# A token stage put into the kernel's own list schedule, with longer two-operand VectorE instructions in place of turns at a shared port

## The chip, the cores and the metric

The kernel runs on one core of a Trainium2 chip. A core has five engines with a queue of instructions each: TensorE (PE in the profile, with its weight loads as PEld), VectorE (DVE), ScalarE (ACT), GpSimd (POOL) and SyncE (SP), which here only starts DMAs. An engine takes its instructions in the order in which the program lists them for it, and waits for another engine through semaphores. On-chip memory is SBUF, and PSUM, which TensorE writes its products to. The metric is the time of one execution on the device in microseconds (us).

## The reference

Four layers are applied in turn to 64 images of 128 channels and 28 x 28 pixels, all in float32: a block of two quantised 3x3 convolutions, self-attention over the pixels, a Mamba layer over the sequence of pixels, and a token Mamba. Only the last is touched. It cuts the 128 channels of each pixel into 8 tokens of 16 channels, and runs a small Mamba over these 8 tokens, for each pixel apart (32 inner channels d, 16 states s):

```
seq = x.transpose(0, 2, 3, 1).reshape(B * H * W, TOKEN_NUM, D_MODEL)
# _mamba(seq): after projection, convolution over the tokens and silu
dt  = softplus(dt @ dt_proj_w.T + dt_proj_b)
dA  = exp(dt[..., None] * A)
dBx = dt[..., None] * Bm[:, :, None, :] * xs[..., None]
h   = dA_t * h + dBx_t                    # step over the 8 tokens
y_t = einsum('nds,ns->nd', h, C_t)
y   = (y + xs * D) * silu(z);  out = y @ out_proj_w.T
```

Then a group norm over 4 groups of channels, silu, and the sum with x.

## The kernel before

The program has three parts one after the other: `conv_block`, `attention_and_mamba` and `token_mamba`. The second already computes the inputs of the token Mamba: xs (`utd`) and silu(z) (`ztd`) are written to device memory for each image.

`token_mamba` has 28 groups k of 14 x 128 pixels. A group is worked in two halves dh of 16 inner channels, and a half in four blocks i of 4 channels (`DB`): 56 halves, 224 blocks. Pixels lie on the 128 partitions, and the free dimension of a block's tile is 4 channels x 16 states x 14 pixel columns = 896 elements.

For each group, `x_proj` (line 1184) computes B and C for all 8 tokens into the tile `BC`: row loads (line 1179), matmuls into `bank` and `dt` (lines 1197 and 1203), copies by ScalarE, a product by VectorE (line 1212) and its sum by TensorE (line 1215). For each half, `delta_u` makes `delta` (softplus) and `u` (delta times xs): 16 ScalarE operations, transposes (line 1242) with copies, four ScalarE passes over 1792 elements, two VectorE passes (lines 1258, 1259), two GpSimd passes (lines 1262, 1263), and `diag` by VectorE (line 1266).

For each block, `exps` fills `a`, the decays of tokens 1 to 7, with 64 ScalarE exponentials of 98 elements. All calls of ScalarE carry line 235 in the profile, that of a helper. `a` has two buffers. `block` runs the recurrence with the state `h` in PSUM, one buffer: GpSimd makes the seven inputs `db` (line 1296, five buffers) and two products (lines 1307 and 1309); VectorE makes the first `h` (line 1308) and then, token by token, multiplies by `a` (line 1311), multiplies by C into `a` or `late` (line 1313) and adds `db` (line 1315). TensorE sums over the states into `y` (lines 1318, 1320 and 1322), ScalarE copies `y` to `ysb`. For each half, `gate` transposes back (line 1333), gates with VectorE and GpSimd (lines 1338 and 1339), exchanges halves through memory (`ygd`), projects (line 1347) and copies to the image `xr` (line 1357). `finish_image` does the group norm and the rest for images that are complete.

The loop at the end of `token_mamba` writes these parts down interleaved: pieces of the last half's `gate`, of the next group's `x_proj` and the next half's `delta_u`, the exponentials of the next block, then the block itself. The order on each engine is made from this by the framework's own scheduler (`tile.TileContext(nc, schedule_with_timeline_sim=True)`).

`attention_and_mamba` is ordered otherwise. There every call goes to a `Plan`, which records it as a `Step`. `add` finds what a step depends on from the parts of tiles that it reads and writes, `cost` (line 372) gives it a duration in us, a lag until others see the result, and whether it takes the port that VectorE and GpSimd share. `order` (line 399) is a list schedule: each engine picks, among its first 32 ready steps by rank, the first that can start within a given patience of the soonest; steps under `first()` have their rank lowered by a lead. A shared step can't start before the last shared step has ended (`port`): these are the turns. Buffers are taken in the order of the program, except PSUM tiles named `bank`. `issue` runs it for 12 pairs of lead and patience (`TRIED`), takes the shortest, and writes the instructions down in that order (line 479), as they are to stay.

Of the kernel before, what the change touches and what calls it, by code (L numbers as in the profile page):

```python
# [19 lines left out]
ALU = mybir.AluOpType  # L20
# [245 lines left out]
class Plan:  # L266
# [12 lines left out]
    def __init__(self, tc):  # L279
        self.tc = tc  # L280
        self.steps, self.access, self.slots, self.group, self.leading = [], {}, {}, None, False
        for e in self.ENGINES:
            setattr(self, e, Recorder(self, e))
# [88 lines left out]
    def cost(self, engine, method, outs, ins, args, kw):  # L372
# [5 lines left out]
        if engine == "tensor":  # L378
            if kw.get("is_transpose"):
                return 0.18, False, 0.25  # L380
            if outs[0].partition_size() == 32 or ins[0].partition_size() == 16:
                return 0.03 + 0.0005 * n, False, 0.25
            return 0.06 + 0.0023 * n, False, 0.25
        if engine == "gpsimd":
            return 0.2 + 0.0023 * n, True, 0.07
        if engine == "scalar":
            if not outs:
                return 1.28, False, 0.07
            a = outs[0]
            us = 0.2 + 0.00093 * n * (1.8 if len(a.ap) > 2 and abs(a.ap[-1][0]) > 1 else 1.0)  # L390
            return us + (0.2 if "accum_out" in kw else 0.0), False, 0.07
        two = len([a for a in big if a.space == SBUF]) > 1
        if method == "tensor_tensor_scan":
            return 0.18 + (0.0024 if two else 0.0021) * n, False, 0.07
        if method == "tensor_scalar" and outs[0].space == SBUF:
            return 0.14 + 0.00053 * n, True, 0.07
# [101 lines left out]
def attention_and_mamba(tc, tables, x, c2d, s2, b2x15, x2d, utd, ztd, pk3, pk4, vec, v, ident, eps):  # L498
# [11 lines left out]
    with ExitStack() as ctx:  # L510
# [99 lines left out]
        plan = Plan(tc)  # L610
# [473 lines left out]
def token_mamba(tc, tables, x2d, utd, ztd, pk4, v, ident, eps, out, NB):  # L1084
# [17 lines left out]
    with ExitStack() as ctx:  # L1102
        dram = ctx.enter_context(dram)
        wp = ctx.enter_context(tc.tile_pool(name="w4", bufs=1))
# [3 lines left out]
        ap = ctx.enter_context(tc.tile_pool(name="a4", bufs=2))  # L1108
        p2 = ctx.enter_context(tc.tile_pool(name="p4", bufs=2))
        p1 = ctx.enter_context(tc.tile_pool(name="p4b", bufs=1))  # L1110
        db = ctx.enter_context(tc.tile_pool(name="db4", bufs=5))
        cp = ctx.enter_context(tc.tile_pool(name="c4", bufs=4))
        xrp = ctx.enter_context(tc.tile_pool(name="xr4", bufs=4))
        ps = ctx.enter_context(tc.tile_pool(name="ps4", bufs=3, space=PSUM))
        psd = ctx.enter_context(tc.tile_pool(name="psd4", bufs=1, space=PSUM))
        psh = ctx.enter_context(tc.tile_pool(name="psh4", bufs=1, space=PSUM))
        psy = ctx.enter_context(tc.tile_pool(name="psy4", bufs=2, space=PSUM))
# [13 lines left out]
        act = tables.act  # L1131
        act(A, w("Alog"), AF.Exp)
        nc.vector.tensor_scalar(A, A, -1.0, None, ALU.mult)

# [5 lines left out]
        def finish_image(b):  # L1140
            xo = xr.pop(b)
            stats = p2.tile([C, 2, 6], F32, name="stats")
            for h in range(2):
                nc.vector.bn_stats(stats[:, h, :], xo[:, h * HT : (h + 1) * HT])
            mv = p2.tile([C, 2], F32, name="mv")
            nc.vector.bn_aggr(mv, stats.rearrange("p n s -> p (n s)"))
            acc = bank()
            nc.tensor.matmul(acc[:, 0:1], lhsT=grp, rhs=mv[:, 0:1], start=True, stop=True)
# [5 lines left out]
            nc.tensor.matmul(acc2[:, 0:1], lhsT=grp, rhs=sm[:, 1:2], start=True, stop=True)  # L1154
# [6 lines left out]
            nc.sync.dma_start(res, x2d[b])  # L1161
# [7 lines left out]
            nc.gpsimd.tensor_tensor(xo, xo, e, ALU.mult)  # L1169
            nc.gpsimd.tensor_tensor(res, res, xo, ALU.add)  # L1170
            nc.sync.dma_start(out[b], res)

        def load_rows(src, k, dh, g, n):
# [3 lines left out]
            for b in range(lo // T, (hi - 1) // T + 1):  # L1177
                p, q = max(lo, b * T), min(hi, (b + 1) * T)
                nc.sync.dma_start(t[:, p - lo : q - lo], src[b][:, dh, p - b * T : q - b * T])
# [4 lines left out]
        def x_proj(k):  # L1184
# [5 lines left out]
            for g, n in chunks:  # L1190
                uts = [load_rows(utd, k, dh, g, n) for dh in range(2)]
                for g2 in range(0, n, 2):
                    two = bank()
                    for j in range(2):
                        at = slice((g2 + j) * C, (g2 + j + 1) * C)
                        for dh in range(2):
                            nc.tensor.matmul(  # L1197
                                two.rearrange("p (c j) -> p c j", j=2)[:, :, j],
                                lhsT=uts[dh][:, at], rhs=w("BDx", dh * 256, (dh + 1) * 256),
                                start=(j == 0 and dh == 0), stop=(j == 1 and dh == 1),  # L1200
                            )
                        for dh in range(2):
                            nc.tensor.matmul(  # L1203
                                dt_ps[:, :, g + g2 + j], lhsT=uts[dh][:, at], rhs=w("BDt", dh * NK, (dh + 1) * NK),
                                start=(g + g2 + j == 0 and dh == 0), stop=(g + g2 + j == G - 1 and dh == 1),
                            )
# [3 lines left out]
            nc.vector.tensor_copy(small[:, 0].rearrange("p t g -> p (t g)"), acc[:, : NK * G])  # L1210
            prod = p1.tile([C, NK, NS, G], F32, name="w1")
            nc.vector.tensor_tensor(prod, BC[:, :, :NS, :], BC[:, :, NS:, :], ALU.mult)
            acc = bank()
            for i in range(NS):
                nc.tensor.matmul(
                    acc[:, : NK * G].rearrange("p (t g) -> p t g", g=G), lhsT=ident, rhs=prod[:, :, i, :],
                    start=(i == 0), stop=(i == NS - 1),
                )
            nc.vector.tensor_copy(small[:, 1].rearrange("p t g -> p (t g)"), acc[:, : NK * G])
# [7 lines left out]
        def delta_u(k, dh):  # L1227
# [9 lines left out]
            for g, n in chunks:  # L1237
# [3 lines left out]
                for j in range(n):  # L1241
                    nc.tensor.matmul(
                        acc4[:, :, j], lhsT=ut[:, j * C : (j + 1) * C], rhs=ident, is_transpose=True,
                        start=(j == 0), stop=(j == n - 1), skip_group_check=True,
                    )
# [12 lines left out]
            nc.vector.scalar_tensor_tensor(e_, w_, 1.0, e_, ALU.subtract, ALU.subtract)  # L1258
            nc.vector.scalar_tensor_tensor(v_, v_, 0.0, e_, ALU.max, ALU.subtract)
            yield  # L1260
            act(w_, w_, AF.Ln)
            nc.gpsimd.tensor_tensor(v_, v_, w_, ALU.add)
            nc.gpsimd.tensor_tensor(u_, v_, u_, ALU.mult)
            yield
            diag = p1.tile([C, NK, ND, G], F32, name="diag")
            nc.vector.tensor_tensor(diag, u, of_tg(small[:, 1]), ALU.mult)
            half[k, dh] = delta, u, diag

        def exps(k, dh, i):
            delta = half[k, dh][0]  # L1270
            a = ap.tile([C, NK - 1, DB, NS, G], F32, name="a")
            for d in range(DB):
                for n in range(NS):
                    col = (dh * ND + i * DB + d) * NS + n
                    act(a[:, :, d, n, :], delta[:, 1:, i * DB + d, :], AF.Exp, scale=A[:, col : col + 1])
            return a

        def block(k, dh, i, a, ysb):
# [15 lines left out]
            def inject(t):  # L1294
                x = db.tile([C, DB, NS, G], F32, name="db")
                nc.gpsimd.tensor_tensor(  # L1296
# [10 lines left out]
            nc.gpsimd.tensor_tensor(flat(at(1)), flat(at(1)), flat(h0), ALU.mult)  # L1307
            nc.vector.tensor_tensor(h, flat(at(1)), flat(inject(1)), ALU.add)  # L1308
            nc.gpsimd.tensor_tensor(by_d(at(1)), by_d(at(1)), Cc(1), ALU.mult)  # L1309
            for t in range(2, NK):  # L1310
                nc.vector.tensor_tensor(h, h, flat(at(t)), ALU.mult)  # L1311
                dst = at(t) if t < 6 else late[:, t - 6]
                nc.vector.tensor_tensor(by_d(dst), h_d, Cc(t), ALU.mult)  # L1313
                if t < NK - 1:
                    nc.vector.tensor_tensor(h, h, flat(inject(t)), ALU.add)  # L1315
            y = psy.tile([C, 512], F32, name="y")[:, : NK * DG]
            y3 = y.rearrange("p (t d g) -> p t d g", d=DB, g=G)
            nc.tensor.matmul(y3, lhsT=ident, rhs=diag[:, :, ds, :], start=True, stop=False)
            for n in range(NS):
                nc.tensor.matmul(y3[:, 1:6], lhsT=ident, rhs=a[:, 0:5, :, n, :], start=False, stop=False)  # L1320
            for n in range(NS):
                nc.tensor.matmul(y3[:, 6:8], lhsT=ident, rhs=late[:, :, :, n, :], start=False, stop=(n == NS - 1))  # L1322
            return y3, ysb[:, :, ds, :]

        def gate(k, dh, ysb):

            yf = ysb.rearrange("p t d g -> p (t d) g")
            for g, n in chunks:
# [3 lines left out]
                for j in range(n):  # L1332
                    nc.tensor.matmul(
                        acc[:, j * C : (j + 1) * C], lhsT=yf[:, :, g + j], rhs=ident, is_transpose=True,
                        start=(j == 0), stop=(j == n - 1), skip_group_check=True,
                    )
                yg = cp.tile([C, 512], F32, name="yg", bufs=3)
                nc.vector.scalar_tensor_tensor(yg[:, :m], ut[:, :m], v("DT", dh), acc[:, :m], ALU.mult, ALU.add)
                nc.gpsimd.tensor_tensor(yg[:, :m], yg[:, :m], zt[:, :m], ALU.mult)
                if dh == 0:  # L1340
                    nc.sync.dma_start(ygd[k % 2][:, g * C : g * C + m], yg[:, :m])
                else:
                    yg0 = cp.tile([C, 512], F32, name="yg", bufs=3)
                    nc.sync.dma_start(yg0[:, :m], ygd[k % 2][:, g * C : g * C + m])
                    acc = bank()
                    for i, r in enumerate((yg0, yg)):
                        nc.tensor.matmul(  # L1347
                            acc[:, :m], lhsT=w("BDo", i * C, (i + 1) * C), rhs=r[:, :m], start=(i == 0), stop=(i == 1)
                        )
                    lo = k * PX + g * C  # L1350
                    at = lo
                    while at < lo + m:
# [4 lines left out]
                        nc.vector.tensor_copy(xr[b][:, o : o + c], acc[:, at - lo : at - lo + c])  # L1357
# [19 lines left out]
        for q, (k, dh) in enumerate(halves_):  # L1377
# [4 lines left out]
            for i in range(NBLK):  # L1382
# [11 lines left out]
                y, dst = block(k, dh, i, a, ysb)  # L1394
                act(dst, y, AF.Copy)
# [3 lines left out]
        for _ in ends:  # L1399
            pass  # L1400

# [100 lines left out]
```

## Time and profile before

| | us |
|---|---|
| runs before, median of 3 | 14057.9 (14039.58 to 14059.44) |
| the profiled execution | 14058.7 |
| its span, first to last instruction | 14056.9 |
| token stage, first to last start of line 1308 | 7984.7 to 13985.3 |

| engine | busy us | share of the span |
|---|---|---|
| PE | 10623.3 | 76% |
| DVE | 12350.4 | 88% |
| ACT | 10874.1 | 77% |
| POOL | 11465.4 | 82% |

A profile line of a group reads: line, engine, operation, output tile <- input tiles, output shape <- input shape, number of instructions | busy us, mean ns of one | idle us of the engine just before them <- who ended it. A line of waits reads: engine and instruction that waited <- whom it waited for: us in total, number of times, longest. A line of the view of one source line or tile has the shortest, median and longest duration in ns and the first and last start. A float32 matmul appears as two records, and neighbouring instructions of ScalarE and TensorE overlap, so that the mean of one is longer than busy time over count.

### The profile page before, as it was taken

What the parts mean: (1) busy time and instruction counts of PE and PEld (TensorE: products, weight loads), DVE (VectorE), ACT (ScalarE), POOL (GpSimd) and SP (SyncE); (2) the same over time, 40 slices, a digit from 0 to 9 for tenths busy, and PEclk for the clock granted to TensorE, in tenths of its full rate; (3) what the DMA queues carried; (4) which work ended last, traced back from release to release, by engine and by line L of the source; (5) the groups of instructions that cost most, each with busy time, mean ns of one, the idle gap of its engine ahead of it and who ended that gap; (6) DMA issues with size and microseconds to landing.
All of it is one profiled execution on the core that took longest, in us unless ns stands there. A gap on an engine that the chain in (4) does not pass through costs nothing. (4 is left out here: it accounts for less than half of the span.)

```text
span 14056.9 us, 183402 instructions
## 1 busy us (share of the span) xinstructions
PE 10623.3 (76%) x59522; PEld 7022.5 (50%) x59522; DVE 12350.4 (88%) x12760; ACT 10874.1 (77%) x25936; POOL 11465.4 (82%) x5304
## 2 busy tenths in 40 slices
PE   9978777777777777777777567767767677677776
PEld 5544444444444444444443356555556555565564
DVE  3459999999999999999999788888888888888897
ACT  2357877777777777777777688888888888888886
POOL 0028999888888888898989788888888888888887
PEclk9988888888888888888888788888888888787887
DMA  2434444444444444444443211111111111111111
GB/s 102 147 111 125 126 124 128 130 126 123 123 134 125 121 126 130 129 121 125 130 127 117 77 47 57 46 50 57 49 54 48 52 58 46 49 58 49 52 49 48
DMA packets 711523, 1297.78 MB, mean 92 GB/s; under 512 B 206624, under 2 KB 357536, under 8 KB 710560
## 3 DMA queue, kind: packets, MB, share of 16 engines
q1 hardware_dynamic: 710560, 1286.05, 30.2%
q8 instruction: 469, 7.68, 0.2%
q14 instruction: 494, 4.05, 0.1%
HBM read 954.72 MB, written 330.76 MB: 91 GB/s over the span
## 5 line engine op out<-in xcount | busy, mean ns | idle before, releaser
L235 ACT ACTIVATE a<-delta,A 128x98 f32<-128x98 f32 x14336 | 3966.8, 380 | 512.7 <-PE y L1320 454.2
L479 POOL TENSOR_TENSOR h<-ur,Br 128x784 f32<-128x784 f32 x1920 | 4196.5, 2211 | 148.8 <-PE y L479 133.6
L1296 POOL TENSOR_TENSOR db<-u,BC 128x896 f32<-128x896 f32 x1568 | 3337.2, 2144 | 548.4 <-DVE h L1315 531.0
L1320 PE MATMUL y<-a,ident 128*128 128x280 f32 x7168 | 2083.5, 452 | 815.3 <-DVE a L1313 811.5
L479 DVE TENSOR_TENSOR_SCAN ah<-ah,h 128x392 f32<-128x392 f32 x2304 | 2305.0, 1000 | 60.2 <-ACT ah L479 49.0
L1320 PEld LDWEIGHTS y<-a,ident 128*128 128x128 f32 x7168 | 1549.1, 220 | 1371.4 <-POOL db L1296 582.9
L479 DVE TENSOR_TENSOR_SCAN h<-a,h 128x784 f32<-128x784 f32 x768 | 1935.6, 2525 | 99.8 <-ACT a L479 50.2
L479 ACT ACTIVATE ah<-dr,A 128x392 f32<-128x392 f32 x2304 | 1326.3, 589 | 615.1 <-DVE ah L479 601.4
L479 POOL TENSOR_TENSOR h<-h,Cr 128x784 f32<-128x784 f32 x640 | 1361.4, 2131 | 356.1 <-DVE h L479 349.2
L1311 DVE TENSOR_TENSOR h<-h,a 128x896 f32<-128x896 f32 x1344 | 1475.4, 1098 | 39.0
L479 DVE TENSOR_TENSOR h<-ah,Cr 128x392 f32<-128x392 f32 x2304 | 1303.7, 566 | 72.9
L479 PE MATMUL y<-h,fold 128*32 128x98 f32 (+1 forms) x12288 | 1019.9, 421 | 396.7 <-DVE h L479 370.4
L1315 DVE TENSOR_TENSOR h<-h,db 128x896 f32<-128x896 f32 x1120 | 1230.1, 1098 | 68.0 <-POOL db L1296 0.5
L479 PEld LDWEIGHTS bank<-vt,et 112*112 112x112 f32 x6272 | 890.8, 212 | 233.8 <-ACT et L479 91.8
L1313 DVE TENSOR_TENSOR a<-h,BC 128x896 f32<-128x896 f32 x896 | 976.1, 1089 | 25.5
L479 PE MATMUL bank<-vt,et 112*112 112x128 f32 x6272 | 966.3, 317 | 5.1 <-ACT et L479 3.0
L479 POOL TENSOR_TENSOR xn<-s,sq 128x784 f32<-128x784 f32 x64 | 135.9, 2123 | 1017.3 <-ACT sq L479 961.3
L1322 PEld LDWEIGHTS y<-late,ident 128*128 128x128 f32 x7168 | 839.5, 192 | 38.9 <-DVE late L1313 20.6
L1322 PE MATMUL y<-late,ident 128*128 128x112 f32 x7168 | 844.4, 274 | 16.7 <-DVE late L1313 16.6
L479 PEld LDWEIGHTS y<-h,fold 128*32 128x32 f32 x12288 | 379.3, 121 | 923.8 <-DVE h L479 439.2
L479 ACT ACTIVATE a<-dr,A 128x784 f32<-128x784 f32 x768 | 718.6, 944 | 154.2 <-DVE h L479 152.5
L1308 DVE TENSOR_TENSOR h<-a,db 128x896 f32<-128x896 f32 x224 | 394.1, 1759 | 388.4 <-POOL a L1307 381.0
(213 smaller groups left out, 20996.5 us busy)
## 6 DMA issues: line engine op xcount, KB each, us to landing
Br<-bcd SPq DMA_DIRECT2D x1536, 98.0 KB, 2.4
Cr<-bcd SPq DMA_DIRECT2D x1536, 98.0 KB, 2.4
dr<-dud SPq DMA_DIRECT2D x1280, 98.0 KB, 2.3
ur<-dud SPq DMA_DIRECT2D x1280, 98.0 KB, 2.3
utd<-tok SPq DMA_DIRECT2D x128, 392.0 KB, 2.7
ztd<-tok SPq DMA_DIRECT2D x128, 392.0 KB, 3.7
rows<-utd SPq DMA_DIRECT2D x192, 256.0 KB, 2.7
xt<-in_x SPq DMA_DIRECT2D x32, 784.0 KB, 4.4
```

The lines of the kernel that those rows point to most:

```text
L235: ins = self.tc.nc.scalar.activation(*args, **kw)
L479: last = getattr(getattr(nc, engine), method)(*args, **kw)
L1296: nc.gpsimd.tensor_tensor(x, of_dg(du[:, t, ds, :]), BC[:, t, :NS, :].unsqueeze(1).broadcast_to([C, DB, NS, G]), ALU.mult)
L1308: nc.vector.tensor_tensor(h, flat(at(1)), flat(inject(1)), ALU.add)
L1311: nc.vector.tensor_tensor(h, h, flat(at(t)), ALU.mult)
L1313: nc.vector.tensor_tensor(by_d(dst), h_d, Cc(t), ALU.mult)
L1315: nc.vector.tensor_tensor(h, h, flat(inject(t)), ALU.add)
L1320: nc.tensor.matmul(y3[:, 1:6], lhsT=ident, rhs=a[:, 0:5, :, n, :], start=False, stop=False)
L1322: nc.tensor.matmul(y3[:, 6:8], lhsT=ident, rhs=late[:, :, :, n, :], start=False, stop=(n == NS - 1))
```

## The change

All calls of `token_mamba` from the load of the first rows on go to a `Plan` of their own, and all its pools are the plan's. The instructions, their operands and their buffers are the same. The setup (weights `pk`, `A`, `grp`) stays outside the plan. Some calls are grouped with `together()`, so that the schedule moves them as one step: the matmuls of a bank, of a `y` (sixteen and sixteen), and four exponentials each. A block and the copy of its `y` stand under `first()`. The plan takes three new arguments: the cost of TensorE per column, that of GpSimd per element, and whether there are turns. The Mamba stage passes the values that stood there before; the token stage passes 0.0019, 0.0022 and False. With False, GpSimd's operations take no port, and a VectorE instruction with two operands in SBUF costs 0.2 + 0.0015 us per element in place of 0.14 + 0.00107. ScalarE operations under 100 elements get a cost of their own.

```
-    def __init__(self, tc):
-        self.tc = tc
+    def __init__(self, tc, column, element, turns):
+        self.tc, self.column, self.element, self.turns = tc, column, element, turns
...
-            return 0.06 + 0.0023 * n, False, 0.25
+            return 0.06 + self.column * n, False, 0.25
         if engine == "gpsimd":
-            return 0.2 + 0.0023 * n, True, 0.07
+            return 0.2 + self.element * n, self.turns, 0.07
...
             a = outs[0]
+            if n < 100:
+                return 0.175 + 0.001 * n, False, 0.07
...
+        if two and not self.turns:
+            return 0.2 + 0.0015 * n, False, 0.07
...
-        plan = Plan(tc)
+        plan = Plan(tc, 0.0023, 0.0023, True)
...
     with ExitStack() as ctx:
         dram = ctx.enter_context(dram)
+        plan = Plan(tc, 0.0019, 0.0022, False)
...
-        ap = ctx.enter_context(tc.tile_pool(name="a4", bufs=2))
+        ap = plan.pool(ctx.enter_context(tc.tile_pool(name="a4", bufs=2)), 2)
...
-        act = tables.act
-        act(A, w("Alog"), AF.Exp)
+        tables.act(A, w("Alog"), AF.Exp)
         nc.vector.tensor_scalar(A, A, -1.0, None, ALU.mult)
+
+        act = plan.scalar.activation
...
             for d in range(DB):
-                for n in range(NS):
-                    col = (dh * ND + i * DB + d) * NS + n
-                    act(a[:, :, d, n, :], delta[:, 1:, i * DB + d, :], AF.Exp, scale=A[:, col : col + 1])
+                for n0 in range(0, NS, 4):
+                    with plan.together():
+                        for n in range(n0, n0 + 4):
+                            col = (dh * ND + i * DB + d) * NS + n
+                            act(a[:, :, d, n, :], delta[:, 1:, i * DB + d, :], AF.Exp, scale=A[:, col : col + 1])
...
             h0 = inject(0)
-            nc.gpsimd.tensor_tensor(flat(at(1)), flat(at(1)), flat(h0), ALU.mult)
-            nc.vector.tensor_tensor(h, flat(at(1)), flat(inject(1)), ALU.add)
-            nc.gpsimd.tensor_tensor(by_d(at(1)), by_d(at(1)), Cc(1), ALU.mult)
+            plan.gpsimd.tensor_tensor(flat(at(1)), flat(at(1)), flat(h0), ALU.mult)
+            plan.vector.tensor_tensor(h, flat(at(1)), flat(inject(1)), ALU.add)
+            plan.gpsimd.tensor_tensor(by_d(at(1)), by_d(at(1)), Cc(1), ALU.mult)
...
-            for n in range(NS):
-                nc.tensor.matmul(y3[:, 1:6], lhsT=ident, rhs=a[:, 0:5, :, n, :], start=False, stop=False)
+            with plan.together():
+                for n in range(NS):
+                    plan.tensor.matmul(y3[:, 1:6], lhsT=ident, rhs=a[:, 0:5, :, n, :], start=False, stop=False)
...
-                y, dst = block(k, dh, i, a, ysb)
-                act(dst, y, AF.Copy)
+                with plan.first():
+                    y, dst = block(k, dh, i, a, ysb)
+                    act(dst, y, AF.Copy)
...
         for _ in ends:
             pass
+        plan.issue()
```

The remaining calls of the stage change from `nc.` to `plan.` in the same way.

## The prediction

> **What bounds the kernel now.** I read the page first: its slices show two regimes, with the border near 7.9 ms of the span of 14056.9 us (profiled execution 14058.7 us, so 1.8 us lie around the span; median of the runs 14057.9 us). Then the busy time by stretch, in which the columns after the length are PE, PEld, DVE, ACT and POOL, then granted clock and DMA. The first line is the attention and Mamba stage, which already runs in the list schedule; this is how it fills its engines:
>
> ```profile
> 2000.00:4000.00 2000.00, 1554.39 (x9750) 882.27 (x9743) 1931.25 (x2139) 1564.46 (x2556) 1785.34 (x811) 0.86 0.43 127
> ```
>
> The token stage, from its first block to its last, its head before and its tail behind:
>
> ```profile
> 7893.00:7985.00 92.00, 64.42 (x296) 51.08 (x296) 12.27 (x17) 66.01 (x151) 21.60 (x9) 0.78 0.32 100
> 7985.00:13985.00 6000.00, 4312.11 (x20677) 3419.61 (x20678) 5288.12 (x4829) 5089.04 (x16642) 5215.43 (x2459) 0.81 0.17 51
> 13985.00:14057.00 72.00, 31.78 (x148) 23.52 (x146) 28.22 (x36) 15.30 (x35) 22.59 (x14) 0.72 0.13 41
> ```
>
> DVE is 96.6% busy in the first regime. In the token stage DVE, POOL and ACT stand at 88, 87 and 85%: none is full. The view of line 1308, which opens each of the 224 blocks, gives the period:
>
> ```profile
> L1308 DVE TENSOR_TENSOR h<-a,db x224: 1073/1168/8558, 7984.7 to 13985.3; 128x896 f32<-128x896 f32 x112
> ```
>
> (13985.3 - 7984.7)/223 = **26.91 us per block**. The waits between 8400 and 13900 us (204 blocks; columns: total, times, longest) show a ring:
>
> ```profile
> PE y L1320 <- DVE a L1313: 689.6, 116, 20.5
> POOL db L1296 <- DVE h L1315: 481.9, 323, 5.3
> ...
> ACT a L235 <- PE y L1320: 403.5, 94, 14.2
> DVE h L1308 <- POOL a L1307: 339.7, 98, 12.0
> ...
> ACT BC L235 <- PE bank L1197: 183.6, 68, 9.2
> ```
>
> ACT waits for an `a` buffer that PE still reads (1.98 us a block), PE for the last product of the block, DVE for the first product of the next one (1.67 us), which needs all 64 exponentials. Work is always there; the order brings it at the wrong time.
>
> **What the Trainium skill says.** "SBUF — State Buffer", section "Who interferes with whom": a VectorE instruction with two SBUF inputs contends with a GpSimd instruction that reads SBUF, and the loser is blocked for the whole of the other; with at most one SBUF input it doesn't contend. The trace agrees with both. Line 1311 (one operand in PSUM) takes 1078 to 1100 ns whatever POOL does. Line 1308 (both in SBUF) takes 1082 to 8558 ns, and one meeting reads:
>
> ```profile
> 10865.33 1.10 DVE L1308 TENSOR_TENSOR h<-a,db 128x896 f32<-128x896 f32 x1 [1.85 <-POOL a L1307]
> 10865.37 2.86 POOL L1296 TENSOR_TENSOR db<-u,BC 128x896 f32<-128x896 f32 x1
> ```
>
> POOL's operation, 1942 ns in the median, grew by 0.92 us. "Perfetto Trace Analysis", section "Optimization Strategy": the same gap again and again on an engine that should be full can mean too few buffers. Here that is `a` with two; whether it binds is worked out below.
>
> **The work of one block.** From the same 204 blocks, by line:
>
> ```profile
> L1308 DVE TENSOR_TENSOR h<-a,db 128x896 f32<-128x896 f32 x204 | 356.0, 1745 | 346.3 <-POOL a L1307 339.7
> L1258 DVE SCALAR_TENSOR_TENSOR e<-w,e 128x1792 f32<-128x1792 f32 x51 | 145.0, 2842 | 13.0 <-ACT w L235 13.0
> ...
> L1212 DVE TENSOR_TENSOR w<-BC 128x1792 f32<-128x1792 f32 x25 | 68.5, 2741 | 1.3 <-ACT BC L235 1.3
> ```
>
> - DVE: lines 1311, 1315 and 1313 make 3794.2 us, 18.60 a block. The two-input ones (1308, 1258, 1259, 1266, 1212) make 356.0 + 145.0 + 139.8 + 144.7 + 68.5 = 854.0 us, 4.19 a block; the rest 1.44. Sum **24.2**. Alone (shortest of their views: 1.082, and 2.015 for the large ones) the two-input ones would take 2.84, so 1.35 us a block is waiting at the port, 0.72 us for each of 1.87.
> - POOL: the groups sum to 4842.7 us, 23.7 a block; at their undisturbed durations (1.942 for line 1296, 2.06 and 2.07 for 1307 and 1309, 3.97 for 1262 and 1263, 1.83 for 1169 and 1170, line 1339 left at its mean of 1.22) 21.95.
> - The port: 21.95 + 2.84 = **24.8 us a block** if no meeting overlaps. That is 92% of 26.91.
> - ACT: 5089.04/223 = 22.8. PE: 19.3.
>
> So DVE and the port each set a floor near 24.5 us, ACT one 1.7 us lower; the order alone costs 2 to 2.5 us a block.
>
> **The change, part by part.**
> 1. *Instructions.* None is added or taken away: every call of the token stage goes to the recorder with the same operands. DMAs are the same. Cost: 0.
> 2. *Order.* The framework's order gives way to the list schedule, the cheapest of twelve by its own costs. The ring: an `a` buffer is held for 64 exponentials (64 x 0.277 = 17.7 us, busy over count), line 1307 (2.1), line 1308 (1.75), the products to step 5 (3 x 3.29 + 2.19 = 12.05) and PE's sixteen pairs (1886.8/204 = 9.2): 42.8 us. With two buffers that allows a period of 21.4, so the ring doesn't bind by itself; at 25.65 it leaves 8.5 us over two blocks for what gets between. The list schedule ranks the block's steps up to 60 ahead, which keeps it short.
> 3. *Costs.* Are the new ones those of the chip? PE 0.06 + 0.0019 x 280 = 0.592, measured 0.578 (1886.8/3264); POOL 2.17 against 2.14; one exponential 0.273 against 0.277; two-input DVE 1.54 and 2.89 against 1.75 and 2.74 to 2.84. Misses: the diagonal matmul 0.91 against 1.39 (284.4/204), the 8-column ones 0.08 against 0.26, delta's bias 0.30 against 0.39. Per block that is 0.5 + 0.6 us on PE, which has 6 us to spare, and 0.3 us on ACT. The late pairs are over-costed by 0.6. So errors nearly cancel.
> 4. *No turns.* The schedule lets a two-input DVE instruction and a POOL instruction run at once; the chip doesn't. The planned order then meets waits where they fall. Unknown of the change: the wait for each. From below 0 (the port happens to be free; the costs allow for 0.44, 1.54 less 1.10); from above a whole POOL operation, 1.94. I take 0.85, a little above today's 0.72, since POOL will be busier: 23.7/25.65 = 92% against 87% now.
> 5. *Grouping* four exponentials, a pair-of-banks group or sixteen matmuls: at most 1.1 us on ACT and 9.2 us on PE in one piece. ACT's pieces are hidden behind the DVE chain of 20 us; a copy queued behind PE's sixteen waits up to 9.2 us, as it does now (longest wait 9.2). If that cover is gone, one such wait in each half of four blocks is 2.3 us a block: it belongs to the range.
> 6. *Head.* SP now issues the first row loads at 7892.9, ahead of the last token stores at 7914.7 to 7917.1; in the recorded order they stand behind these. PE's first matmul, at 7916.3, moves to about 7917.1 + 0.5 + 2.7 (landing of such a load) = 7920: +5 us. The bound is 0 to 10.
> 7. *Mamba stage:* same arguments as before, and no activation under 100 elements there, so 0. *Tail* (72 us): drain of the last gate, 0 within 15.
>
> **Sum.** DVE 22.87 + 1.87 x 0.85 = 24.46 us. How full will it run? 96.6% in the Mamba stage under the same list; here three engines are close together, so I take 95.4%: 25.64, say 25.65. Check at the port: 24.8/25.65 = 97%. Change: (26.91 - 25.65) x 223 = 281 us gained, 5 lost: 14058.7 - 276 = 13782.7; the median stands 0.8 below the profiled execution, so **13782 us**. Its own range, period 25.3 to 26.6 with head and tail: 13705 to 13990.
>
> **Rivals.**
> - *The port full.* DVE with today's waits at 96.4%: 24.22/0.964 = 25.1, 14058 - 223 x 1.8 + 5 = about 13660; the floor of the port, 24.8, is 13592. For it: in the Mamba stage, between 3000 and 6000 us, POOL's undisturbed operations (about 2336 us) and the two-input DVE ones (at least 645) fill 99% of the time. Against: there ACT has 22% to spare, here 10.
> - *Little or nothing.* The `a` waits stay, since ACT's copies wait for PE as now and exponentials queue behind them. Period 26.6 to 27.05: about 14000 to 14090, middle 14035. For it: the 345 us that ACT waits for PE's banks (183.6 for `BC`, 161.4 for `u`); against: the 8.5 us of room.
> - *Slower: the missing turns.* POOL issues one operation after another, DVE comes second each time and loses a full 1.94 us: 22.87 + 1.87 x 1.94 = 26.5, and with 1.5 us idle 28.0, so +243 + 5 = 14306 us. It decides from a mean wait of (26.91 - 1.5 - 22.87)/1.87 = 1.36 us, against 0.72 now. For it: waits to 8.56 us on line 1308 today, when both 4-us operations of lines 1262 and 1263 come first. Against: where DVE waits for line 1307 it is first at the port (10865.33 before 10865.37).
> - That it reorders the Mamba stage too: its stretch would no longer show 1931 us of 2000. I see no way in the costs.
>
> **How the numbers follow.** My forecast 0.48; port full 0.15; little or nothing 0.10, half of it within 0.2% (28 us, about what a measurement of this kernel can tell from no change); slower 0.27, its core the missing turns. Faster 0.48 + 0.15 + 0.05 = 0.68, same 0.05, slower 0.27. The range, 13610 to 14180, leaves out the last of the port's case (0.04) and slower ones beyond a period of 27.45 (0.13).
>
> **What would show it.** Right: 1308 spaced 25.3 to 26.6 us; DVE at 94 to 96% and POOL above 91% in the token stage; ACT's wait for PE on `a` below 200 us; two-input means below 1.95 us (1308) and 3.1 us (1258). Wrong: 1308 above 2.4 us on the mean (missing turns), or ACT below 86% with PE waits of today's size (little or nothing). What would break it most: an order that fits the costs but stalls in-order queues at each half's start, where delta, PE copies and POOL's 8 us follow one another.

## The result and the profile after

The changed kernel takes 13983.1 us in the median of 5 runs (13959.1 to 13995.8), against 14057.9 us before: a ratio of **0.9948, 95% interval 0.9933 to 0.9964**. That is 75 us gained, where 276 were forecast. The profiled execution took 13966.6 us with a span of 13964.7 us.

All calls that a plan issues carry line 485 now, in the Mamba stage and in the token stage alike, so the readings go by tiles: `h<-a,db` is the first product of a block (line 1308 before), POOL's `a<-a,db` the one in front of it (1307). Busy time by stretch; columns after the length: PE, PEld, DVE, ACT, POOL, then granted clock and DMA. The second line is the token stage from its first block to its last:

```profile
2000.00:4000.00 2000.00, 1567.63 (x9734) 888.76 (x9731) 1912.41 (x2133) 1559.60 (x2552) 1780.03 (x809) 0.85 0.43 127
7983.70:13895.80 5912.10, 4279.38 (x20720) 3452.32 (x20721) 5433.57 (x4830) 5118.50 (x16645) 5183.91 (x2458) 0.83 0.18 52
13895.80:13965.00 69.20, 33.25 (x145) 23.18 (x143) 29.71 (x36) 17.30 (x35) 25.09 (x15) 0.71 0.14 42
```

The Mamba stage is as it was (DVE 1912 us of 2000). In the token stage DVE stands at 92% (88 before), POOL at 88 and ACT at 87. The first product's own view has the period and the meetings at the port (count: shortest/median/longest ns, first and last start):

```profile
L485 DVE TENSOR_TENSOR h<-a,db x224: 1082/2716/4835, 7983.7 to 13895.8; 128x896 f32<-128x896 f32 x112
```

(13895.8 - 7983.7)/223 = **26.51 us per block**, from 26.91; 25.65 was forecast. The median of this instruction went from 1168 to 2716 ns: in more than half of the blocks it now waits out most of a GpSimd operation. Two-operand instructions by group, between 8400 and 13800 us (203 blocks; count | busy us, mean ns | idle before):

```profile
L485 DVE TENSOR_TENSOR h<-a,db 128x896 f32<-128x896 f32 x203 | 441.8, 2176 | 171.4 <-POOL a L485 140.1 <-POOL db L485 25.0
L485 DVE TENSOR_TENSOR diag<-u,small 128x1792 f32<-128x1792 f32 x50 | 170.3, 3406 | 0.0
L485 DVE SCALAR_TENSOR_TENSOR delta<-delta,e 128x1792 f32<-128x1792 f32 x51 | 170.3, 3339 | 1.7
```

And ACT's waits in the same stretch:

```profile
ACT a L485 <- PE y L485: 469.3, 114, 10.0
ACT a L485 <- issue: 86.2, 35, 4.3
...
ACT BC L485 <- PE bank L485: 5.4, 3, 2.5
```

The copies out of PSUM no longer wait (BC 183.6 us before, 5.4 now), and DVE waits 0.69 us a block for the first product in place of 1.67. But ACT's wait for an `a` buffer grew from 1.98 to 2.31 us a block. The new order cleared most of these waits, but not that for the ring: the two buffers of `a`, each of which ScalarE may fill again only when TensorE has read it.

Per block, from the groups over the whole stretch between first and last block (sums over 223; idle is the period less the sum). A sum of groups counts the overlap of neighbouring records twice; by stretch DVE is busy 5433.57/223 = 24.37 us of the 26.51, where the groups give 24.71:

| us per block | before | forecast | after |
|---|---|---|---|
| two-operand DVE, with waits at the port | 4.15 | 4.43 | 4.71 |
| other DVE | 20.01 | 20.03 | 20.00 |
| DVE idle | 2.75 | 1.19 | 1.80 |
| period | 26.91 | 25.65 | 26.51 |

### The profile page after: what moved, and what is told of

Read it like the earlier page. It is cut to its first block, busy times and chain, and to the rows that moved or that the text cites. A ratio compares the mean times of both kernels' runs of the same rounds, so it can differ in the third digit from the quotient of the medians.

```text
span 13964.7 us, 183713 instructions
## 1 busy us (share of the span) xinstructions
PE 10617.7 (76%) x59522; PEld 7069.8 (51%) x59522; DVE 12469.0 (89%) x12760; ACT 10892.0 (78%) x25936; POOL 11444.2 (82%) x5304
## 5 line engine op out<-in xcount | busy, mean ns | idle before, releaser
L485 ACT ACTIVATE a<-delta,A 128x98 f32<-128x98 f32 x14336 | 3904.8, 366 | 757.1 <-PE y L485 512.4
L485 POOL TENSOR_TENSOR db<-u,BC 128x896 f32<-128x896 f32 x1568 | 3279.2, 2117 | 127.7 <-DVE h L485 120.4
L485 DVE TENSOR_TENSOR_SCAN h<-a,h 128x784 f32<-128x784 f32 x768 | 1904.9, 2485 | 116.2 <-ACT a L485 61.3
L485 DVE TENSOR_TENSOR a<-h,BC 128x896 f32<-128x896 f32 x896 | 976.9, 1090 | 28.8
L485 POOL TENSOR_TENSOR a<-a,db 128x896 f32<-128x896 f32 x224 | 531.1, 2371 | 307.9 <-issue 240.7
```

Source lines behind the costliest of these rows:

```text
L485: last = getattr(getattr(nc, engine), method)(*args, **kw)
```

## The experiments

Theories: the **port** (the plan lets VectorE's two-operand instructions and GpSimd's run at once, so the meetings cost what is missing), the **ring** (the two buffers of `a` bind), and **order luck** (any list order drifts from its plan, and ends near the same). The plan is made anew for each of these kernels, so every edit also moves the order. Ratios are to the kernel before, with 95% intervals. The wait at the port is what the two-operand groups take above their undisturbed 2.84 us a block, over 1.87 instructions.

### Turns, with the chip's undisturbed durations

```
-        plan = Plan(tc, 0.0019, 0.0022, False)
+        plan = Plan(tc, 0.0019, 0.00195, True)
```

> The changed kernel, but its token stage is planned with turns at the port and with durations that are not stretched by waiting: GpSimd 0.2 + 0.00195 us per element (1.95 us for 896), two-operand VectorE 1.10 and 2.06 us. Port theory (the order is made for a chip without the lock, so two-operand VectorE instructions meet GpSimd ones: 1.02 us of wait each in the changed kernel, 0.72 before): the mean wait falls below 0.6 us, the block period from 26.5 to 25.7 to 26.2 us, 13810 to 13920 us. Ring theory (the two buffers of a bind, ScalarE waits for TensorE): the order hardly matters, 13960 to 14010 us. Order-luck theory (any list order ends near the same, in-order queues drift apart from the plan): 13930 to 14030 us with waits at the port about as in the changed kernel.

Three costs change here: the turns, GpSimd's duration, and that of two-operand instructions, which is the long one only without turns (same_cost, below, changes this one alone).

Measured: 14067.8 us, ratio 1.0015 (1.0007 to 1.0024), slower than the changed kernel. No theory had that. There are 4.41 us of two-operand work a block, a wait at the port of (4.41 - 2.84)/1.87 = 0.84 us in place of (4.71 - 2.84)/1.87 = 1.00 (the expectation's 1.02 is from the shorter stretch); the port theory asked for less than 0.6. But the period is 26.96 us, so DVE idles 2.54 us. ACT shows where (between 8400 and 13600 us, 192 blocks):

```profile
ACT a L485 <- PE y L485: 554.5, 111, 10.1
```

That is 2.89 us a block, against 2.31. There is less waiting at the port, and the kernel is slower: the port theory falls as the one cause of the missing 200 us.

### The list schedule with the Mamba stage's costs

```
-        plan = Plan(tc, 0.0019, 0.0022, False)
+        plan = Plan(tc, 0.0023, 0.0023, True)
```

> The list schedule alone: the token stage planned with the constants and the turns of the Mamba stage (0.0023 for both, turns), all else as in the changed kernel. It tells what the new costs without turns are worth. Port theory: with turns the plan keeps the two apart, but TensorE and GpSimd are over-costed (0.70 us for a pair measured at 0.58, 2.26 for 1.94), so that the plan fills the queues for a slower chip: 13950 to 14100 us, wait per two-operand instruction below 0.72 us. If the missing turns are what costs: faster than the changed kernel, below 13950 us. If the new costs are the whole gain: at or above the kernel before, 14060 us or more.

Measured: 14335.4 us, ratio 1.0202 (1.0187 to 1.0217); the period is 28.22 us and the wait at the port 0.71. So the list schedule as it was is 2% slower than the framework's order. Between this and the run above stand only two cost constants, 268 us apart: the fitted durations bring the list schedule from 2% slower to about level with the framework's order. The number of the branch "new costs are the whole gain" is met, though with turns the fitted durations alone gain nothing over the kernel before.

### The ring made longer

```
-                dst = at(t) if t < 6 else late[:, t - 6]
+                dst = at(t) if t < 7 else late[:, t - 7]
-            late = p1.tile([C, 2, DB, NS, G], F32, name="late")
+            late = p1.tile([C, 1, DB, NS, G], F32, name="late")
-                    plan.tensor.matmul(y3[:, 1:6], lhsT=ident, rhs=a[:, 0:5, :, n, :], ...)
+                    plan.tensor.matmul(y3[:, 1:7], lhsT=ident, rhs=a[:, 0:6, :, n, :], ...)
-                    plan.tensor.matmul(y3[:, 6:8], ...)
+                    plan.tensor.matmul(y3[:, 7:8], ...)
```

> The changed kernel with one more product kept in a: step 6 goes to a and no longer to late, so TensorE reads a 3.3 us later and for 336 in place of 280 columns (the late matmuls get 56 columns less); the same sums, the same work on VectorE and GpSimd. An a buffer is held some 5 us longer. Ring theory: half of that comes back for each block, about 2 us times 224: +300 to +550 us, 14280 to 14530 us. Port theory: the ring has room, +0 to +100 us, 13980 to 14080 us.

Measured: 14349.6 us, ratio 1.0216 (1.0198 to 1.0233), 366 us above the changed kernel, with the same arithmetic on all engines. The period went from 26.51 to 28.14 us:

```profile
L485 DVE TENSOR_TENSOR h<-a,db x224: 1099/2805/2843, 7982.6 to 14258.8; 128x896 f32<-128x896 f32 x112
```

DVE's wait for the first product rose to 305.6 us in 184 blocks:

```profile
ACT a L485 <- PE y L485: 503.8, 85, 11.6
...
DVE h L485 <- POOL a L485: 305.6, 79, 10.4
```

DVE's wait is 1.66 us a block, against 0.69, and ACT's for the buffer 2.74, against 2.31. The two-operand work fell to 4.46 us, so it isn't the port that lengthens the block. This is the ring theory's number; room of 8.5 us would have swallowed it.

### One operand fewer in the first product

```
-            plan.vector.tensor_tensor(h, flat(at(1)), flat(inject(1)), ALU.add)
+            inject(1)
+            plan.vector.tensor_scalar(h, flat(at(1)), 1.0, None, ALU.mult)
```

It leaves out the input of token 1 in the recurrence.

> The changed kernel with the first product of each block read from one operand: h is copied from a with a factor of 1, and the input of token 1 is still made by GpSimd, but not added (left out: that one term of the recurrence). One of 1.87 two-operand VectorE instructions in a block loses its meeting at the port: 1.1 us less on VectorE, and as much less on GpSimd. Port theory: 0.8 to 1.5 us a block, -180 to -330 us, 13650 to 13800 us. Ring theory: the ring gets shorter by about 1.1 us for two blocks, -60 to -130 us, 13850 to 13920 us. If neither: within 30 us of 13983.

Measured: 13822.2 us, ratio 0.9835 (0.982 to 0.985), 161 us below the changed kernel; period 25.87. The instruction takes 1090 ns on the mean:

```profile
L485 DVE TENSOR_SCALAR h<-a x224: 1071/1094/1097, 7986.7 to 13755.0; 128x896 f32<-128x896 f32 x112
```

The time falls between the two expectations: DVE has 1.27 us less to do (23.44 against 24.71), but the period fell by 0.64 only. Idle time rose by as much as was missing, and ACT's wait for `a` was still 416.1 us in 200 blocks, 2.08 us each. What was taken off the engine with the most work came back by half. That the ring keeps the rest fits this wait, but isn't shown alone: the plan also has a shorter cost for the instruction here (1.10 us for 1.54).

### The ring made shorter

The step-5 product goes to `late`. `A` is computed in place in `pk`, to make room for the wider `late`.

```
-                dst = at(t) if t < 6 else late[:, t - 6]
+                dst = at(t) if t < 5 else late[:, t - 5]
-            late = p1.tile([C, 2, DB, NS, G], F32, name="late")
+            late = p1.tile([C, 3, DB, NS, G], F32, name="late")
-                    plan.tensor.matmul(y3[:, 1:6], lhsT=ident, rhs=a[:, 0:5, :, n, :], ...)
+                    plan.tensor.matmul(y3[:, 1:5], lhsT=ident, rhs=a[:, 0:4, :, n, :], ...)
-                    plan.tensor.matmul(y3[:, 6:8], ...)
+                    plan.tensor.matmul(y3[:, 5:8], ...)
...
-        A = wp.tile([C, 512], F32, name="A")
+        A = w("Alog")
```

> The changed kernel with the product of step 5 kept in late and no longer in a (late is 3 steps wide, A takes the place of its weights in pk to make room); the same sums and the same work on VectorE and GpSimd. TensorE can start to read a 3.3 us earlier and has 224 columns in place of 280 in its sixteen pairs. An a buffer is held about 4 to 5 us less. Ring theory: the ring is tight for about two thirds of the blocks (it gave 1.63 us a block for 5 us more), so 0.7 to 1.3 us a block come back, -150 to -300 us, 13680 to 13830 us; ScalarE's wait for TensorE on a falls below 300 us. VectorE theory (it is full between the waits of its own, and lengthening the ring only made a new limit): within 40 us of 13983.

Measured: **13689.5 us, ratio 0.9744 (0.973 to 0.9759)**, 294 us below the changed kernel: more than what the forecast had missed. The period is 25.27 us:

```profile
L485 DVE TENSOR_TENSOR h<-a,db x224: 1084/1102/2851, 7980.6 to 13616.0; 128x896 f32<-128x896 f32 x112
```

The token stage by stretch, and ACT's waits (8400 to 13600 us):

```profile
7980.00:13616.00 5636.00, 4157.55 (x20727) 3696.03 (x20727) 5336.13 (x4830) 5123.01 (x16647) 5035.68 (x2458) 0.86 0.19 54
```

```profile
ACT a L485 <- DVE h L485: 188.6, 65, 5.5
ACT sm L485 <- PE bank L485: 77.8, 30, 8.3
```

DVE is at 94.7%. ACT's wait for PE on `a` is all but gone (11.9 us); what is left is mainly a wait for VectorE's last reading of `a`, 0.92 us a block over 205 blocks. Of the 1.24 us that a block became shorter, 0.83 is idle time of DVE (0.97 by the groups, from 1.80) and 0.40 less waiting at the port (two-operand work of 4.31 us, a wait of 0.79 us an instruction). The order moved too: in the second block of a half the 64 exponentials, with what comes between, take 20.0 us on the mean against 25.2 in the changed kernel. How much of the gain is the shorter hold itself, and how much the new order that it allows, wasn't separated.

The control has the second edit alone, `A` in place:

> A control: the changed kernel with A computed in place in pk, the edit that made room in ring_short and before_short, and nothing else. All theories: within 20 us of the changed kernel, a ratio of 0.994 to 0.996 to the kernel before. If it differs by more, the gain of ring_short isn't the ring's alone.

Measured: 13992.8 us, ratio 0.9953 (0.9939 to 0.9966). The edit that makes room does nothing that can be told.

The same shortening in the framework's own order, without the list schedule:

> The kernel before, in the framework's own order, with the same edit as ring_short. If the ring binds in that order too: -100 to -300 us, 13750 to 13950 us. If what it loses is the order itself (products brought at the wrong time, 1.3 us in the median between the exponentials and line 1307): within 60 us of the kernel before.

Measured: 13868.7 us, ratio 0.9874 (0.9858 to 0.9891), 182 us below the median of the runs of before beside it. The ring held that order too; its waits between 8400 and 13600 us:

```profile
ACT a L235 <- DVE h L1311: 225.3, 69, 9.7
ACT BC L235 <- PE bank L1197: 211.6, 72, 9.6
ACT u L235 <- PE bank L1242: 103.5, 27, 8.9
```

The copies' waits stay, under the framework's order, and so does the time of the exponentials in the second block of a half (20.0 us, from 19.9): here the gain comes without that shift of side work. The list schedule is worth 0.5% with the ring as it was (0.9948 against 1), and 1.3% with the shorter one (0.9744 against 0.9874).

### What the cost of two-operand instructions and the lead are worth

```
         if two and not self.turns:
-            return 0.2 + 0.0015 * n, False, 0.07
+            return 0.14 + 0.00107 * n, False, 0.07
```

> The changed kernel without the longer cost of two-operand VectorE instructions: no turns, and 1.10 and 2.06 us for them as with one operand. It isolates the last words of the change. If the longer cost keeps the plan near the chip: +30 to +120 us, 14010 to 14100 us. If the chip's waits at the port undo the plan anyway: within 30 us of 13983. The mean wait at the port stays at 0.9 to 1.1 us.

Measured: 14036.6 us, ratio 0.9992 (0.9983 to 1.0). So the longer cost is worth 0.44%, most of the changed kernel's gain; the wait at the port is 0.80 us, lower than with it and lower than expected. ACT's waits (8400 to 13600 us, 193 blocks):

```profile
ACT a L485 <- PE y L485: 602.6, 112, 11.2
```

That is 3.12 us a block, against 2.31 in the changed kernel and 2.89 in turns_fit. So neither the lower wait at the port nor the longer wait for `a` of turns_fit needs the turns: the shorter cost alone shows both. What the longer cost buys isn't fewer meetings; it may be room in the plan.

Lead 0 alone:

```
         plan = Plan(tc, 0.0019, 0.0022, False)
+        plan.TRIED = [(0, patience) for patience in (0.05, 0.12, 0.2, 0.3)]
```

> The changed kernel with its token stage scheduled with a lead of 0 alone (the changed kernel takes the best of 0, 30 and 60): blocks get no rank ahead of the side work. If the planned order carries over to the chip: side work gets between the chain of a block, the chain to the last product in a grows from 13.5 us to 15 or more, +80 to +200 us, 14060 to 14180 us. If in-order queues drift from the plan so far that its choice doesn't matter: within 40 us of 13983.

Measured: 14025.7 us, ratio 0.9983 (0.9976 to 0.999), 0.35% above the changed kernel. That is between the two expectations, and the mechanism named isn't seen: the chain to the last product in `a` averages 13.85 us, against 13.49. Order luck as a theory falls, though: five orders of the same work span 2.5% (0.9948 to 1.0202). Most of that is turns_old; the four with costs near the chip's span 0.7%, a third of what ring_short gained over the changed kernel.

### The two port questions again, with the shorter ring

> ring_short planned with turns at the port and undisturbed durations (GpSimd 1.95 us for 896 elements, two-operand VectorE 1.10 and 2.06 us), as turns_fit was against the changed kernel. There the wait per two-operand instruction fell from 1.02 to 0.84 us and the kernel still came out 85 us slower, with more of ScalarE's wait on a. If the ring hid what the turns are worth: at or below ring_short, 13600 to 13690 us, wait at the port below 0.7 us. If the turns themselves make the worse order (GpSimd held back in the plan where the chip would let it run ahead): above ring_short, 13720 to 13850 us.

Measured: 13718.9 us, between the two expectations, ratio 0.9758 (0.9742 to 0.9775), against 0.9744 (0.973 to 0.9759) of ring_short. The intervals overlap: with the shorter ring, turns in place of the longer cost neither help nor harm by an amount that can be told. The wait at the port is 0.73 us.

> ring_short without the longer cost of two-operand VectorE instructions (1.10 and 2.06 us, no turns), as same_cost was against the changed kernel, where it cost 54 us. If the longer cost was worth something only because an early planned chain makes the ring wait: within 25 us of ring_short, 13665 to 13715 us. If it is worth the same without the ring: 13720 to 13770 us.

Measured: 13768.4 us, ratio 0.9793 (0.9778 to 0.9807), 0.5% above ring_short. The longer cost is worth the same without the old ring; the theory that it served the ring falls. Between short_turns and short_same stand only the turns and GpSimd's duration, and there the turns are faster by 0.4%; with the old ring the same pair (turns_fit against same_cost) has them slower by 0.2%.

## Why the prediction was wrong

The direction and the place held, and the time lies within the range; the size did not, and one step of the working failed. Of what was to show the forecast right, the period (26.51, at the edge of 25.3 to 26.6) was met; DVE at 94 to 96% (92), POOL above 91% (88), ACT's wait below 200 us (469.3) and a mean below 1.95 us for the first product (2.18) were not; the large one that was to stay below 3.1 us did (2.48).

**Step 2, the ring, is the step that failed.** It summed the parts at their own durations, 42.8 us, found 8.5 us of room, and concluded that the ring doesn't bind. With it longer the kernel lost 2.7%, with it shorter it gained 2.1% (1.0216 and 0.9744, over 0.9948). The trace of the changed kernel, followed from the first write of a buffer to its next (means over blocks 4 to 219), and two others beside it:

| us | step 2 | before | after | ring_short |
|---|---|---|---|---|
| 64 exponentials, with what comes between | 17.7 | 19.0 | 20.3 | 20.1 |
| to GpSimd's first product, and that | 2.1 | 4.0 | 2.9 | 3.4 |
| to DVE's first product (DVE at other work) | 0 | 1.9 | 3.1 | 4.0 |
| first product | 1.75 | 1.8 | 2.2 | 1.7 |
| the chain: from there to the end of DVE's last product in `a` | 12.05 | 14.9 | 13.5 | 9.6 |
| to PE, and its sixteen pairs | 9.2 | 11.4 | 10.5 | 8.0 |
| to the first exponential two blocks on | 0 | 1.0 | 0.7 | 4.0 |
| sum = two periods | 42.8 | 54.0 | 53.2 | 50.7 |

With two buffers the sum is two periods by construction. What tells that the ring binds, beside ACT's waits, is the last line: after the change ScalarE fills a buffer again 0.7 us after it was let go, in ring_short 4.0 us after. The column of the kernel before had the 54.0 us already.

Even without the 3.1 us in which DVE is mostly at other work (the end of the last block, and side work: what is done for the half or the group), the hold is 50.1 us after the change, 7.3 above step 2: 2.6 us of other ScalarE work between the exponentials, 2.6 of handovers (0.5 + 1.4 + 0.7), 1.4 of side work and gaps in the chain, 0.7 on the two first products at the port. At the forecast period that leaves 51.3 - 50.1 = 1.2 us of the 8.5, on the mean, and less than nothing where side work comes in a lump. That is most often in the second block of a half. One such place, on ACT:

```profile
10832.49 2.23 ACT L485 ACTIVATE a<-delta,A 128x98 f32<-128x98 f32 x8
10841.94 2.25 ACT L485 ACTIVATE a<-delta,A 128x98 f32<-128x98 f32 x8 [7.22 <-PE y L485]
10844.10 5.29 ACT L485 ACTIVATE delta<-small,pk 128x112 f32<-128x112 f32 x14
...
10855.53 7.58 ACT L485 ACTIVATE a<-delta,A 128x98 f32<-128x98 f32 x28
...
10866.23 6.50 ACT L485 ACTIVATE a<-delta,A 128x98 f32<-128x98 f32 x24
```

and the two engines behind it:

```profile
10872.86 2.08 POOL L485 TENSOR_TENSOR a<-a,db 128x896 f32<-128x896 f32 x1 [0.69 <-POOL db L485]
...
10874.98 1.10 DVE L485 TENSOR_TENSOR h<-a,db 128x896 f32<-128x896 f32 x1 [5.18 <-POOL a L485]
```

ACT stands idle for 7.22 us until PE lets go of the buffer. Then 11.4 us of side work (10844.10 to 10855.53) come in among the exponentials, which so take from 10841.94 to 10872.6, and DVE is out of work for 5.18 us. Taken from the trace for blocks 8 to 215, the gap ahead of `h<-a,db` is 2.62 us on the mean in the second block of a half, and 0.1 to 0.6 in the other three.

**How full DVE runs** (95.4% assumed, from the Mamba stage) is where this enters the sum: 24.71/26.51 = 93.2%, so 1.80 us of idle in place of 1.19. Those 0.61 us make 136 us over 223 blocks, of 192 for the whole difference in the period (0.86 x 223). The 95.4% also mixed two measures: the 96.6% behind it is a share by stretch, and the 24.46 us are a sum of groups, which before was 0.45 us above the stretch (24.16 against 5288.12/223 = 23.71). With one measure the working gives (24.46 - 0.45)/0.954 = 25.2 us, further from what was measured, so this slip isn't what failed.

**Step 4, the wait at the port**, had its mechanism right and its size too small: 1.00 us for each of 1.87 instructions where 0.85 was taken, 0.28 us a block, 62 us. The bound of 1.94 held for the mean; a single first product took up to 4.84 us. It doesn't decide alone: turns_old and turns_fit, with less of it (0.71 and 0.84), were slower, and ring_short (0.79) faster.

**Step 3**, that the new costs are those of the chip, held, and matters more than was said: with turns, the older two constants are at 1.0202 and fitted ones at 1.0015. **Step 5** named the copies behind PE's sixteen pairs as a risk of 2.3 us a block; they all but stopped waiting (BC and `u` together 345 us before, some 10 after). **Step 6**, +5 us at the head, was wrong in what comes last: the first row loads still start at 7893.2, ahead of the token stores, and PE's first matmul, at 7917.03, waits for the load of `pk`, which landed at 7916.8 (7916.1 before). The first block starts at 7983.7, 1.0 us earlier. **Steps 1 and 7** and the tail (69 us against 72) held.

**Of the rivals**, "little or nothing" had the right object, the `a` waits, with the wrong reason, copies behind PE; its 14000 us is nearer to the 13983 measured than the forecast's 13782. "The missing turns" asked for a mean wait of 1.36 us and met 1.00. "The port full" is the nearest description of ring_short, with 25.27 us where it had 25.1, but by another way: a buffer let go earlier.

Open: why the shorter cost of two-operand instructions, alone in same_cost and with turns in turns_fit, lengthens the wait for `a` with the old ring, and why turns cost a little with the old ring and gain a little with the shorter one. That the plan places the blocks' side work differently is a reading of the same waits, and wasn't tried apart. That the longer cost works as room in the plan was argued from its two comparisons, not shown by an experiment on room alone.

## What to carry to other kernels

Before trusting the room in a double buffer, follow one buffer through the trace from its first write to the next one, with every wait and every foreign instruction between: the sum of the bare durations (42.8 us here) was a fifth below what the queues made of it (53.2). Here, with three engines near 90%, order and hold time were worth more together than apart: moving one product out of the long-held buffer gave 1.3% in the old order and 2.1% in the new one (0.9744/0.9948). Fit a schedule's costs to the trace first: two constants made 1.9% here (1.0202 against 1.0015).

## What the runs showed of the hardware

The first product, with one operand from SBUF, takes 1071 to 1097 ns in all 224 blocks of one_input, beside a GpSimd that is 88% busy (5055.63 of 5768.3 us), and 2176 ns on the mean with two, in the changed kernel: there the meetings at the port cost VectorE on the mean about as much as the instruction itself. Unexpected was that more waiting at the port can go with a faster kernel: 1.00 us an instruction and 13983 us after the change, 0.80 us and 14037 us in same_cost, 0.84 us and 14068 us in turns_fit.
